# PSUM banks sorted by the engine that empties them, and rounds of segment attention and retention in another order

## Chip, core and metric

The kernel runs on one core of one Trainium2 chip. The metric is the device time of one execution in microseconds. Five engines work in parallel, each through its own instruction stream in order: TensorE (PE, matmuls and transposes, with its weight loads shown as PEld), VectorE (DVE), ScalarE (ACT), GpSimd (POOL) and SyncE (SP, DMA issue). Matmul results land in PSUM, which has eight banks; an engine has to empty a bank before TensorE writes the next result to it.

## What is computed

A four layer decoder on x of shape (16, 256, 128) with a context of shape (16, 64, 128). Each layer is attention (of a different kind each time), cross attention to the context, and a feed forward part, each followed by a residual add and layer norm. All of it is float32. The parts that the change touches, in the reference's words, cut to what matters:

```python
# layer 0, 2, 3: cross attention, 16 heads of 8, softmax over the 64 context positions
out = softmax(q @ k.T / sqrt(8)) @ v ;  x = layernorm(x + out @ Wo + bo)
# layer 1: attention in segments of 64, plus strided keys of two neighbour segments on either side
out = _attn(q, k, v)
for off in (1, 2):
    for sign in (-1, 1):
        out = out + where(valid, _attn(q, kd[n], vd[n]) * w, 0)
# layer 2, feed forward: int8 product
acc = dot(round(x / lhs_scale), round(rhs / rhs_scale));  x = layernorm(x + acc * lhs_scale * rhs_scale)
# layer 3: retention
qk = (qr @ kr.T) * mask;  out = (qk / clip(abs(sum(qk)), 1)) @ v
x = layernorm(x + (silu(x @ Wg + bg) * groupnorm(out)) @ Wo + bo)
```

## The kernel before

x stays in SBUF as 8 groups g of 512 tokens (two of the 16 batches b each): `xt` holds tokens on the partitions, `xT` the transpose. `transposed(g)` (L350) turns a group: four TensorE transposes to a bank, one copy to `xT` on ACT. Matmuls go through `mm` (L336), transposes through `tr` (L343), so nearly all TensorE work is shown under these two lines; the name of the output tile tells it apart.

Each stage is one `with s.banks(...)` block. `banks(tag=(n, k))` gives n buffers of k banks to a tag, and `bank(tag)` takes the next one in turn: a matmul that writes it waits for the last reader of what was there before. `in_order()` keeps TensorE's instructions in program order, so a waiting matmul holds up all that is behind it. `deferring()` puts off the last part of a layer norm until `settle()`.

**Segment attention** (`layer_a1`, the loop at L992). One round handles one batch. Its parts: own scores (segment keys; tag sc, exponentials on ACT as `eo`), far sums, sums (tags den, num), far scores (exponentials `e`), values (tag m, added on DVE to `vxs`, L904), project (tag m, q or k of a later group, evacuated by ACT), scaled (scores of the reciprocal, multiplied on DVE into `e`, L963), transposed, out (tag m, then the tail: DVE `r`, layer norm), and keys (POOL, `kb` L888). There is one m bank.

**Cross attention** (`layer_x0` for layer 0, which also hosts a recurrence by `side`, and two further users in layers 2 and 3). One round per batch: scores, then queries, sums, keys, out, values and transposed in some rounds. Banks before: sc 2 of 2 banks, nd few, m 4 - few, with few = 1 in layer 0 and 2 in the others. m takes values (emptied by DVE, `vx`), queries (DVE, `qT`), out (DVE, `r`), the recurrence's turn (DVE) and transposed (ACT, `xT`). Layer 3 begins with a mask row loaded by DMA, reduced on DVE to `nmx` (L1750).

**Int8 product and retention** (`Int8Product`, `layer_a3`). The loop runs over batches n with two half rounds t = 0, 1; g = n // 2. Four half rounds make a period, called H0 (n even, t 0), H1 (n even, t 1), H2 (n odd, t 0), H3 (n odd, t 1) here. Each has the next half's `scores` (tag sc; DVE multiplies into `a`, L1620), `outputs` (tag o), and some of: keys_values (`vz`, DVE), state (a transpose of k, copied by ACT to `kt`), state_product (`st`, DVE L1609), turned (two matmuls, DVE `tq`/`tk` and `ts`), integers (rounding), product (transposes of the rounded group, ACT copy `qT`, matmul, ACT `ys`, POOL, then DVE `r`), scales, gated (two matmuls and two Silu on ACT), normed, finish, transposed. All but scores and outputs use tag m, 3 banks.

Of the kernel before, what the change touches and what calls it, by code (L numbers as in the profile page):

```python
# [222 lines left out]
class Net:  # L223
# [125 lines left out]

    def transposed(self, g, dve=False):  # L350

        ps = self.bank("m" if "m" in self.ps else "ps1")
        for j in range(4):
            self.tr(ps[:, 128 * j:128 * j + 128], self.xt[:, 4 * g + j, :])
        (self.nc.vector.tensor_copy if dve else self.nc.scalar.copy)(self.xT[:, 512 * g:512 * g + 512], ps)  # L355
# [167 lines left out]
def cross_attention(s, wq, wk, wv, wo, bq, bk, bv, finish, mask=None, side=None):  # L523
# [80 lines left out]
    few = 1  # L604
    if side is None:
        side, few = lambda b, late: None, 2
    with s.banks(sc=(2, 2), nd=(few, 1), m=(4 - few, 1)), s.in_order(), s.deferring():
        side(-1, False)
        for g in range(2):
            ps = s.bank("nd")  # L610
            s.mm(ps, wk, s.ctx2[:, 8 * g:8 * g + 8, 0, :])
            evac(s, kT[:, 512 * g:512 * g + 512], ps, bk)
        values(0)
        side(-1, True)
        queries(0)
        keys(0)
        keys(1)
        scores(0)
        for b in range(B + 6):
            if b + 1 < B:  # L620
                scores(b + 1)
            s.settle()
            side(b, False)
            if b % 2 == 0 and b + 2 < B:
                queries(b // 2 + 1)
            if b < B:
                sums(b)
            side(b, True)
            if b + 2 < B:
                keys(b + 2)  # L630
            if b % 2 == 0 and 2 <= b <= B:
                out(b // 2 - 1)
            if b % 4 == 1 and b + 3 < B:
                values(b // 4 + 1)
            if b % 2 == 1 and b >= 5 and b // 2 - 2 < NG:
                s.transposed(b // 2 - 2)
# [223 lines left out]
def layer_a1(s, w):  # L860
# [108 lines left out]
    def far_sums(b):  # L969
        for u in range(2):  # L970
            for i in range(4):
                s.mm(num[b][32 * i:32 * i + 32, 1, :], vxs[b % 2][:, 4, i, 32 * u:32 * u + 32], ed[b][:, i, u, :],
                     u == 0, u == 1)
        oT[b] = s.work("oTn", [128, S], bufs=3)
        nc.vector.tensor_tensor(oT[b], rw[b], num[b][:, 1, :], ALU.add)
# [7 lines left out]
    with s.banks(sc=(2, 2), den=(1, 1), num=(2, 1), m=(1, 1)), s.in_order(), s.deferring():  # L983
        project(q, "qT", 0, w["q"], w["bq"])
        project(k, "kTs", 0, w["k"], w["bk"])
        keys(0)
        keys(1)
        values(0)
        project(q, "qT", 1, w["q"], w["bq"])
        own_scores(0)  # L990
        far_scores(0)
        for b in range(B + 4):  # L992
            if b + 1 < B:
                own_scores(b + 1)
            if 1 <= b <= B:
                far_sums(b - 1)
            if b < B:
                sums(b)
            if b + 1 < B:
                far_scores(b + 1)  # L1000
                values(b + 1)
            s.settle()
            g = (b + 3) // 2
            if g < NG:
                project(*((k, "kTs", g, w["k"], w["bk"]) if b % 2 == 0 else (q, "qT", g, w["q"], w["bq"])))
            if b < B:
                scaled(b)
            if b % 2 == 1 and 3 <= b and b // 2 - 2 >= 0 and b // 2 - 2 < NG:
                s.transposed(b // 2 - 2)
            if b % 2 == 1 and 3 <= b <= B + 1:  # L1010
                out(b // 2 - 1)
            if b + 2 < B:
                keys(b + 2)


def layer_x1(s, w, gate):
# [459 lines left out]
class Int8Product:  # L1476
# [3 lines left out]
    def __init__(self, s, w):  # L1480
        self.s, nc = s, s.nc
        self.idb = s.lp.tile([128, 128], BF, name="idb")
        nc.vector.tensor_copy(self.idb, s.ident)
        self.sw = sw = s.lp.tile([128, D], FP, name="sw")
        nc.gpsimd.partition_all_reduce(sw, w, 128, bass_isa.ReduceOp.absmax)
        nc.vector.tensor_scalar(sw, sw, 1e-12, 1.0 / 127.0, ALU.max, ALU.mult)
        q = s.work("t2", [128, 4, D], bufs=1)[:, 0, :]
        nc.vector.reciprocal(q, sw)
        nc.vector.tensor_tensor(q, q, w, ALU.mult)
        nc.vector.tensor_scalar(q, q, -127.0, None, ALU.max)  # L1490
        nc.vector.tensor_scalar(q, q, 127.0, MAGIC, ALU.min, ALU.add)
        self.qw = s.lp.tile([128, D], BF, name="qw")
        nc.vector.tensor_scalar(self.qw, q, MAGIC, None, ALU.subtract)
        self.xq, self.sx = {}, {}

    def integers(self, g):

# [10 lines left out]
        self.xq[g] = s.work("xq2", [128, 4, D], BF)  # L1508
        nc.vector.tensor_scalar(self.xq[g], t, MAGIC, None, ALU.subtract)

    def product(self, g):
        s, nc = self.s, self.s.nc
        ps = s.bank("m", [128, 4, 128], BF)
        for j in range(4):
            s.tr(ps[:, j, :], self.xq[g][:, j, :], self.idb)
        qT = s.work("qT2", [128, 4, 128], BF)
        nc.scalar.copy(qT, ps)
        y = s.bank("m", [128, 4, D])
        for j in range(4):
            s.mm(y[:, j, :], qT[:, j, :], self.qw)  # L1520
        ys = s.work("ys2", [128, 4, D], bufs=1)
        for j in range(4):
            nc.scalar.activation(ys[:, j, :], y[:, j, :], AF.Identity, scale=self.sx[g][:, j:j + 1])
        nc.gpsimd.tensor_tensor(ys, ys, self.sw.unsqueeze(1).broadcast_to([128, 4, D]), ALU.mult)
        s.tail(g, ys, transpose=False)


def layer_a3(s, w):
# [64 lines left out]
    def state(n):  # L1593

        kk, qb = qk["k", n // 2][:, n % 2, :], qk["q", n // 2][:, n % 2, :]
        ps = s.bank("m")
        s.tr(ps[:, 0:128], kk[:, 0:128])
        kt = s.work("kt", [128, 128])
        nc.scalar.copy(kt, ps[:, 0:128])
        cum = s.work("cum", [128, S])  # L1600
        nc.vector.tensor_tensor_scan(cum, ones, kk, 0.0, ALU.mult, ALU.add)
        nc.gpsimd.tensor_tensor(qks[n % 6], cum, qb, ALU.mult)
        return kt
# [53 lines left out]
        nc.vector.reciprocal(z, z)  # L1657
        return z

    def gated(g):  # L1660
        gates[g] = s.work("gate", [128, 2, 2, S])
        for c in range(2):
            ps = s.bank("m", [128, 2, S])
            s.mm(ps, w["g"][:, 128 * c:128 * c + 128], s.xT[:, 512 * g:512 * g + 512])
            nc.scalar.activation(gates[g][:, :, c, :], ps, AF.Silu, bias=w["bg"][:, c:c + 1])

    def normed(n):
        r = slice(32 * (n % 4 // 2), 32 * (n % 4 // 2) + 32)
# [12 lines left out]
                s.mm(y[:, j, :], gates[g][:, j // 2, c, 128 * (j % 2):128 * (j % 2) + 128], wo[:, c, :], c == 0, c == 1)  # L1681
        s.tail(g, y, s.biased(g, w["r_bo"]), transpose=False)

    with s.banks(sc=(2, 2), o=(1, 1), m=(3, 1)), s.in_order(), s.deferring():
        f2.product(0)
        s.settle()
        f2.integers(2)
        f2.product(1)
        s.transposed(0)
        turned("k", 0, ck, sk)  # L1690
        turned("q", 0, cq, sq)
        f2.integers(3)
        s.settle()
        f2.product(2)
        s.transposed(1)
        keys_values(0)
        kt = state(0)
        scores(0, 0)
        state_product(0, kt)
        for n in range(B + 6):  # L1700
            g = n // 2
            for t in range(2):
                nxt = (n, 1) if t == 0 else (n + 1, 0)
                if nxt[0] < B:
                    scores(*nxt)
                if n < B:
                    outputs(n, t)
                s.settle()
                if t == 0 and n + 1 < B:
                    keys_values(n + 1)  # L1710
                    kt = state(n + 1)
                if t == 1 and n + 1 < B:
                    state_product(n + 1, kt)
                if n % 2 == 0 and g + 1 < NG:
                    turned(*(("k", g + 1, ck, sk) if t == 0 else ("q", g + 1, cq, sq)))
                if n % 2 == 0 and t == 0 and g + 4 < NG:
                    f2.integers(g + 4)
                if n % 2 == 0 and t == 1 and g + 3 < NG:
                    f2.product(g + 3)
                if n % 2 == 1 and t == 0 and g + 2 < NG:  # L1720
                    s.transposed(g + 2)

                if n % 4 == 0 and t == 0 and 4 <= n <= B:
                    rs[n // 4 - 1] = scales(n - 4)
                d = g - 2
                if 0 <= d < NG:
                    if n % 2 == 0 and t == 1:
                        gated(d)
                    if n % 2 == 1:
                        normed(2 * d + t)  # L1730
                if n % 2 == 0 and t == 0 and 0 <= g - 3 < NG:
                    finish(g - 3)
                if n % 2 == 1 and t == 1 and 0 <= g - 3 < NG:
                    s.transposed(g - 3)
# [279 lines left out]
```

## Time and profile before

| | us |
|---|---|
| runs | 2192.61, 2199.82, 2200.99 (median 2199.82) |
| profiled execution | 2195.37, span 2193.6 |

The busy time by engine in the stretches of the stages (us from the span's start):

| stage | stretch | length | PE | DVE | ACT | POOL | PE clock |
|---|---|---|---|---|---|---|---|
| cross attention, layer 0 | 56 to 180 | 124 | 94.2 | 84.9 | 65.8 | 49.1 | 0.87 |
| segment attention | 282 to 541 | 259 | 208.3 | 117.5 | 97.4 | 65.1 | 0.89 |
| cross attention, layer 2 | 1076 to 1178 | 102 | 85.3 | 63.3 | 50.9 | 36.9 | 0.88 |
| int8 product, retention | 1178 to 1490 | 312 | 250.7 | 219.4 | 80.5 | 131.3 | 0.87 |
| cross attention, layer 3 | 1490 to 1605 | 115 | 87.1 | 79.9 | 70.6 | 62.6 | 0.89 |

The other stages, some 1,281 us, are not touched. In lines of the profile, "[1.32 <-DVE vxs L904]" at the end means that the engine stood idle for 1.32 us before the instruction and that the instruction waited last for the one named. In a group's line the figures after the bar are its busy time in us, the mean ns of one instruction, and the idle time just before the group's instructions.

### The profile page before, as it was taken

Reading aid. Unit: us, or ns where it says so; the run is one execution under the profiler, and the core shown is the slowest. Engines: PE = TensorE matmul, PEld = TensorE weight load, DVE = VectorE, ACT = ScalarE, POOL = GpSimd, SP = SyncE. Lnnn points to the kernel's source line nnn. Section 1 sums busy time; section 2 is a strip of 40 time slices with the busy share of each in tenths; the row PEclk is TensorE's granted clock in tenths of the full one; section 3 lists DMA queues with packets and bytes.
Section 4 is the critical chain, followed back from the end, with each engine's and each line's share of the span. In section 5 each row is a group of like instructions: output and inputs, shape, how many; then the busy total and the mean of one; then the engine's idle time right before and its main releaser. Section 6 shows DMA issues by size and latency. Waiting matters only on the chain.

```text
span 2193.6 us, 38398 instructions
## 1 busy us (share of the span) xinstructions
PE 1782.1 (81%) x16059; PEld 1102.1 (50%) x16060; DVE 1131.9 (52%) x2808; ACT 855.2 (39%) x1267; POOL 810.2 (37%) x956
## 2 busy tenths in 40 slices
PE   5784378887899945939895788897879988999998
PEld 2451256655677733625552455664434434555554
DVE  4677624555366665145476777856825543322231
ACT  6465633442333311322354122224756753332231
POOL 2342232221344324764533334435546652211110
PEclk8797569998899965979996889988989999999999
DMA  3000000001011121440000000001000000000000
GB/s 115 4 3 21 1 2 3 3 3 46 1 30 30 62 62 26 86 100 1 6 2 33 1 1 1 2 2 63 2 1 1 2 1 0 6 5 5 5 10 10
DMA packets 45646, 41.52 MB, mean 19 GB/s; under 512 B 6881, under 2 KB 42145, under 8 KB 44833
## 3 DMA queue, kind: packets, MB, share of 16 engines
q1 hardware_dynamic: 35456, 31.22, 4.6%
q0 software_dynamic: 5632, 4.33, 1.5%
q10 hardware_dynamic: 4384, 3.52, 0.5%
q8 instruction: 126, 2.06, 0.4%
q14 instruction: 48, 0.39, 0.1%
HBM read 28.44 MB, written 10.62 MB: 18 GB/s over the span
## 4 chain that ended last, share of the span: by engine, by line
PE 59%; DVE 17%; POOL 9%; issue 7%; ACT 4%; DMA 1%; POOLq 0%; DVEq 0%; ACTq 0%; SPq 0%
PE p L336 14%; PE m L336 13%; PE sc L336 12%; PE y L336 6%; PE nd L336 3%; PE nd L340 3%; POOL rs L383 2%; PE den L340 2%; DVE st L393 2%; PE m L343 2%; POOL acc L1312 2%; PE num L336 2%; DVE r L458 1%; ACT xt L404 1%; DVE e L963 1%
## 5 line engine op out<-in xcount | busy, mean ns | idle before, releaser
L336 PE MATMUL p<-h,w_f 128*128 128x512 f32 x512 | 222.3, 593 | 0.6 <-DVE h L1814 0.6
L381 POOL TENSOR_SCALAR ve<-mv 128x4 f32<-128x4 f32 x128 | 30.8, 241 | 432.3 <-DVE mv L394 429.6
L343 PE MATMUL m<-ident,xt 128*128 128x128 f32 x448 | 87.4, 317 | 95.3 <-ACT xt L404 48.5
L336 PEld LDWEIGHTS p<-h,w_f 128*128 128x128 f32 x512 | 96.9, 190 | 119.9 <-issue 118.0
L1904 ACT ACTIVATE e<-sc 128x1024 f32<-128x1024 f32 x128 | 124.0, 1021 | 61.7 <-PE sc L336 59.5
L383 POOL TENSOR_TENSOR rs<-ve,nhalf 128x4 f32<-128x4 f32 x128 | 133.9, 1046 | 6.3
L336 PE MATMUL sc<-qT,kb 32*128 32x64 f32 (+1 forms) x1792 | 103.8, 356 | 26.9 <-POOL kb L888 7.9
L343 PEld LDWEIGHTS m<-ident,xt 128*128 128x128 f32 x448 | 58.1, 155 | 129.6 <-ACT xt L404 56.8
L393 DVE BATCH_NORM_STATS2 st<-r 128x6 f32<-128x128 f32 x480 | 119.4, 271 | 2.6
L435 POOL TENSOR_TENSOR xb<-xt,r_x 128x512 f32<-128x512 f32 x48 | 61.1, 1276 | 158.5 <-DVE r L1757 72.3
L404 ACT ACTIVATE xt<-r,nm,rs 128x128 f32<-128x128 f32 x176 | 72.5, 484 | 106.9 <-POOL nm L399 106.9
L355 ACT COPY xT<-m 128x512 f32<-128x512 f32 x104 | 59.6, 580 | 132.6 <-PE m L343 132.0
L336 PE MATMUL m<-xT,w_a 128*128 128x512 f32 x144 | 81.9, 684 | 25.5 <-DVE vxs L904 18.6
L336 PEld LDWEIGHTS sc<-qT,kb 32*128 32x128 f32 x1792 | 77.7, 208 | 48.7 <-issue 16.7
L1819 ACT ACTIVATE h<-p,w_f 128x512 f32<-128x512 f32 x64 | 44.0, 687 | 146.8 <-PE p L336 146.7
L1975 DVE RECIPROCAL rcT<-nd 128x256 f32<-128x256 f32 x48 | 83.9, 1749 | 30.7 <-PE nd L336 30.7
L407 DVE TENSOR_SCALAR xt<-r,mv,rs 128x128 f32<-128x128 f32 x208 | 66.7, 382 | 59.6 <-POOL rs L383 59.6
L1825 DVE TENSOR_TENSOR ys<-y,r_f 128x512 f32<-128x512 f32 x8 | 5.5, 692 | 175.4 <-PE y L336 175.4
L1620 DVE TENSOR_TENSOR a<-sc,cst 128x1024 f32<-128x1024 f32 x64 | 75.0, 1208 | 14.3 <-PE sc L336 14.1
L578 ACT ACTIVATE e<-sc 128x1024 f32<-128x1024 f32 x64 | 61.9, 1019 | 49.7 <-PE sc L336 49.7
L394 DVE BATCH_NORM_AGGREGATE mv<-st 128x2 f32<-128x6 f32 x512 | 80.9, 166 | 0.1
L336 PE MATMUL sc<-kb,kTs 32*128 32x512 f32 x512 | 79.0, 652 | 0.0
(425 smaller groups left out, 4116.3 us busy)
## 6 DMA issues: line engine op xcount, KB each, us to landing
acc<-xt SPq DMA_DIRECT2D x16, 256.0 KB, 2.6
mw<-in_moe SPq DMA_DIRECT2D x8, 512.0 KB, 4.2
yx<-acc SPq DMA_DIRECT2D x12, 256.0 KB, 3.4
w_f<-in_w_f SPq DMA_DIRECT2D x1, 2824.0 KB, 10.4
w_x<-in_w_x SPq DMA_DIRECT2D x1, 2336.5 KB, 9.5
xt<-in_x SPq DMA_DIRECT2D x8, 256.0 KB, 7.4
rows<-xn SPq DMA_DIRECT2D x8, 256.0 KB, 2.5
out_x<-xt SPq DMA_DIRECT2D x8, 256.0 KB, 2.3
```

What stands on the lines that cost most here:

```text
L336: self.put(self.nc.tensor.matmul(out=out, lhsT=lhsT, rhs=rhs, start=start, stop=stop))
L340: self.put(self.nc.tensor.matmul(out=out, lhsT=lhsT, rhs=rhs, start=start, stop=stop, skip_group_check=True))
L343: self.put(self.nc.tensor.transpose(out, in_, self.ident if ident is None else ident))
L383: nc.gpsimd.tensor_tensor(rs, ve, self.nhalf[:, :n], ALU.pow)
L393: nc.vector.bn_stats(st[:, j, :], r[:, j, :])
L394: nc.vector.bn_aggr(mv[:, j, :], st[:, j, :])
L404: ins, front = nc.scalar.activation(out[:, j, :], r[:, j, :], AF.Identity, bias=nm[:, j:j + 1], scale=rs[:, j:j + 1]), self.latest
L407: ins, front = nc.vector.tensor_scalar(out[:, j, :], r[:, j, :], mv[:, j, 0:1], rs[:, j:j + 1], ALU.subtract, ALU.mult), self.mark
L578: s.latest = nc.scalar.activation(eu, sc[h], AF.Exp, scale=8 ** -0.5)
L1620: s.mark = nc.vector.tensor_tensor(a[:, h, :, :], sc[h].rearrange("p i j k -> p (i j) k"), tri, ALU.mult)
L1904: nc.scalar.activation(e[:, 2 * h:2 * h + 2, :, :], sc[h], AF.Exp, scale=8 ** -0.5)
L1975: s.nc.vector.reciprocal(rc, nd[:, 1, :])
```

## The change

Three things. In cross attention and retention a second tag t takes the tiles that ACT empties, and m keeps those that DVE empties, with the number of banks divided between them. In the retention loop the int8 product is split: `turn` (transposes and copy) runs in H0, one half round ahead of `product`; and `gated` is split by column half: half 1 stays in H1, half 0 moves to H3 of the pair before, ahead of `transposed` there. In segment attention, project moves from behind values to behind far sums, keys from the end of the round to behind sums, and transposed from the odd rounds (ahead of out) to the following even ones.

```diff
@@ transposed
-        ps = self.bank("m" if "m" in self.ps else "ps1")
+        ps = self.bank("t" if "t" in self.ps else "m")
@@ cross_attention
-    with s.banks(sc=(2, 2), nd=(few, 1), m=(4 - few, 1)), s.in_order(), s.deferring():
+    with s.banks(sc=(2, 2), nd=(few, 1), m=(1, 1), t=(3 - few, 1)), s.in_order(), s.deferring():
@@ layer_a1
-        for b in range(B + 4):
+        for b in range(B + 5):
             if b + 1 < B:
                 own_scores(b + 1)
             if 1 <= b <= B:
                 far_sums(b - 1)
+            g = (b + 3) // 2
+            if g < NG:
+                project(*((k, "kTs", g, w["k"], w["bk"]) if b % 2 == 0 else (q, "qT", g, w["q"], w["bq"])))
             if b < B:
                 sums(b)
+            if b + 2 < B:
+                keys(b + 2)
             if b + 1 < B:
                 far_scores(b + 1)
                 values(b + 1)
             s.settle()
-            g = (b + 3) // 2
-            if g < NG:
-                project(*((k, "kTs", g, w["k"], w["bk"]) if b % 2 == 0 else (q, "qT", g, w["q"], w["bq"])))
             if b < B:
                 scaled(b)
-            if b % 2 == 1 and 3 <= b and b // 2 - 2 >= 0 and b // 2 - 2 < NG:
-                s.transposed(b // 2 - 2)
+            if b % 2 == 0 and 0 <= b // 2 - 3 < NG:
+                s.transposed(b // 2 - 3)
             if b % 2 == 1 and 3 <= b <= B + 1:
                 out(b // 2 - 1)
-            if b + 2 < B:
-                keys(b + 2)
@@ Int8Product
+    def turn(self, g):
+        s, nc = self.s, self.s.nc
+        ps = s.bank("t", [128, 4, 128], BF)
+        for j in range(4):
+            s.tr(ps[:, j, :], self.xq[g][:, j, :], self.idb)
+        self.qT[g] = s.work("qT2", [128, 4, 128], BF)
+        nc.scalar.copy(self.qT[g], ps)
+
     def product(self, g):
-        ps = s.bank("m", [128, 4, 128], BF)
+        y = s.bank("t", [128, 4, D])
         for j in range(4):
-            s.tr(ps[:, j, :], self.xq[g][:, j, :], self.idb)
-        qT = s.work("qT2", [128, 4, 128], BF)
-        nc.scalar.copy(qT, ps)
-        y = s.bank("m", [128, 4, D])
-        for j in range(4):
-            s.mm(y[:, j, :], qT[:, j, :], self.qw)
+            s.mm(y[:, j, :], self.qT[g][:, j, :], self.qw)
@@ layer_a3, state
-        ps = s.bank("m")
+        ps = s.bank("t")
@@ layer_a3, gated
-    def gated(g):
-        gates[g] = s.work("gate", [128, 2, 2, S])
-        for c in range(2):
-            ps = s.bank("m", [128, 2, S])
-            s.mm(ps, w["g"][:, 128 * c:128 * c + 128], s.xT[:, 512 * g:512 * g + 512])
-            nc.scalar.activation(gates[g][:, :, c, :], ps, AF.Silu, bias=w["bg"][:, c:c + 1])
+    def gated(g, c):
+        if c == 0:
+            gates[g] = s.work("gate", [128, 2, 2, S])
+        ps = s.bank("t", [128, 2, S])
+        s.mm(ps, w["g"][:, 128 * c:128 * c + 128], s.xT[:, 512 * g:512 * g + 512])
+        nc.scalar.activation(gates[g][:, :, c, :], ps, AF.Silu, bias=w["bg"][:, c:c + 1])
@@ layer_a3, loop (a turn stands ahead of each product before the loop as well)
-    with s.banks(sc=(2, 2), o=(1, 1), m=(3, 1)), s.in_order(), s.deferring():
+    with s.banks(sc=(2, 2), o=(1, 1), m=(2, 1), t=(1, 1)), s.in_order(), s.deferring():
...
                     turned(*(("k", g + 1, ck, sk) if t == 0 else ("q", g + 1, cq, sq)))
+                if n % 2 == 0 and t == 0 and g + 3 < NG:
+                    f2.turn(g + 3)
...
                     if n % 2 == 0 and t == 1:
-                        gated(d)
+                        gated(d, 1)
                     if n % 2 == 1:
                         normed(2 * d + t)
+                if n % 2 == 1 and t == 1 and 0 <= d + 1 < NG:
+                    gated(d + 1, 0)
                 if n % 2 == 0 and t == 0 and 0 <= g - 3 < NG:
                     finish(g - 3)
                 if n % 2 == 1 and t == 1 and 0 <= g - 3 < NG:
                     s.transposed(g - 3)
```

More of the change, by code (lines that the diff above doesn't have):

```diff
@@ L1493, in __init__ @@
         nc.vector.tensor_scalar(self.qw, q, MAGIC, None, ALU.subtract)
-        self.xq, self.sx = {}, {}
+        self.xq, self.sx, self.qT = {}, {}, {}
     def integers(self, g):
@@ L1682, in finish @@
         s.tail(g, y, s.biased(g, w["r_bo"]), transpose=False)
-    with s.banks(sc=(2, 2), o=(1, 1), m=(3, 1)), s.in_order(), s.deferring():
+    with s.banks(sc=(2, 2), o=(1, 1), m=(2, 1), t=(1, 1)), s.in_order(), s.deferring():
+        f2.turn(0)
         f2.product(0)
@@ L1687, in layer_a3 @@
         f2.integers(2)
+        f2.turn(1)
         f2.product(1)
@@ L1693, in layer_a3 @@
         s.settle()
+        f2.turn(2)
         f2.product(2)
```

## The prediction

> **What bounds it.** I read the page first: its chain of work and its costliest groups.
>
> ```profile
> PE 59%; DVE 17%; POOL 9%; issue 7%; ACT 4%; DMA 1%; POOLq 0%; DVEq 0%; ACTq 0%; SPq 0%
> L336 PE MATMUL sc<-qT,kb 32*128 32x64 f32 (+1 forms) x1792 | 103.8, 356 | 26.9 <-POOL kb L888 7.9
> L336 PE MATMUL m<-xT,w_a 128*128 128x512 f32 x144 | 81.9, 684 | 25.5 <-DVE vxs L904 18.6
> L1620 DVE TENSOR_TENSOR a<-sc,cst 128x1024 f32<-128x1024 f32 x64 | 75.0, 1208 | 14.3 <-PE sc L336 14.1
> ```
>
> TensorE carries most of the chain, but the matmuls do not change (each engine has the same instructions after as before, and no moved step issues a DMA). What can change is where TensorE stands still for a PSUM bank, and which wait then ends last. The third line names one such wait: 18.6 us for DVE's vxs, all in the segment attention. So I went stage by stage: busy time by stretch, the waits of that stretch, and the timeline of one steady round.
>
> **Segment attention (a1), 13 steady rounds of 13.5 to 14 us.** The timeline of one round (start, duration):
>
> ```profile
> 398.10 1.15 PE L336 MATMUL sc<-qT,kbd 32*128 32x256 f32 x16
> 399.27 1.94 ACT L929 ACTIVATE e<-sc 128x1024 f32<-128x1024 f32 x2 [3.15 <-PE sc L336]
> ...
> 400.14 1.13 DVE L904 TENSOR_TENSOR vxs<-m,r_a 64x160 f32<-64x160 f32 x4 [1.00 <-PE m L336]
> ...
> 401.41 1.10 PE L336 MATMUL m<-xT,w_a 128*128 128x512 f32 x2 [1.32 <-DVE vxs L904]
> 402.44 1.15 PE L336 MATMUL sc<-rcT,w_a 32*128 32x256 f32 x16
> ...
> 403.62 2.35 DVE L963 TENSOR_TENSOR e<-e,sc 128x1024 f32<-128x1024 f32 x2 [2.35 <-PE sc L336]
> ```
>
> Far scores, values, a wait of 1.32 for the one m bank, project, scaled scores; then DVE multiplies (e) and the next own scores wait for its end. Far scores to e is 5.52 us. The change puts project behind far_sums: its 1.10 us of PE stay, but outside this stretch, which should be compared as 5.52 - 1.10 = 4.42. The new order already stands in the rounds that have no project (b = 13):
>
> ```profile
> 495.94 1.15 PE L336 MATMUL sc<-qT,kbd 32*128 32x256 f32 x16
> ...
> 499.11 1.13 PE L336 MATMUL sc<-rcT,w_a 32*128 32x256 f32 x12 [0.21 <-ACT e L929]
> 499.89 2.35 DVE L963 TENSOR_TENSOR e<-e,sc 128x1024 f32<-128x1024 f32 x2 [0.78 <-PE sc L336]
> ```
>
> That is 3.95. So not the 1.32 is won: scaled now waits for ACT's exponentials, and 4.42 - 3.95 = 0.47 a round remains; 13 rounds (b = 0 to 12): **-6.1**. Project now runs where m is free; its evacuation and the POOL kb it feeds come some 8 us earlier in the round. The 7.9 us of kb waits in the second line above lie beside the wait for e that follows them, so nothing is taken for them.
>
> Odd rounds end with transposed, ACT's copy and out, and the own scores start behind out, not behind e: 419.93 against e's end at 419.48, and 503.07 against 502.24 for b = 13. With transposed in the even rounds, where the wait for e covers it, out follows scaled at once: 4 x 0.5 + 0.9 = **-2.9**. In the tail the old order ran transposed(6) at 531.11 to 532.74, its copy, and only then out(7) at 533.42; now out(7) needs only oTn, ready at 528.54. What follows (norm, transposed(7), the first x1 matmul at 541.59) comes 4.9 earlier less some queueing: **-4.5**. Sum for a1 **-13.5**; ends -8 (only half of the 0.47 and half of the tail) and -16 (kb waits counted once).
>
> **Cross attention banks.** In x0, m goes from 3 banks to 1 and t gets 2; turn, queries, out and values, all emptied by DVE, now queue for one bank. Queries(b = 2, 6, 10) must wait for DVE's vx: done at 115.82 where queries started at 115.25, so 0.6 each; and turn waits for the r of out (0.3), with nd behind it. 3 x 0.6 plus 0.2: **+2**, ends 0 (TensorE waits for xT or oTn anyway: 8.2 and 7.5 us of such waits in this stage) and +3.5.
>
> In x2 and x3, m goes from 2 to 1 and t gets 1. Queries(b = 6, 10) waited 0.6 for ACT's xT copy only because of its bank; that goes, about 0.9 each with the next instruction's lead. Against it, out now waits for qT's evacuation (x2, b = 8: qT ends 1131.94, out started 1131.28, +0.7; in x3 1530.28 against 1530.39, nothing). x2: -1.8 + 0.7, and at b = 4 up to 1.15 more (qT ends 1110.31, out started 1109.16): **0** (ends -1, +1.5); x3: **-1.9** (ends -2.5, 0).
>
> At x3's start the instruction order of DVE changes too. Before:
>
> ```profile
> 1497.88 1.22 DVE L1750 TENSOR_REDUCE nmx<-e 128x16 f32<-128x1024 f32 x1 [6.98 <-DMA e<-in_mk]
> ...
> 1499.24 2.63 DVE L554 TENSOR_TENSOR vx<-m,r_x 64x64 f32<-64x64 f32 x8
> ...
> 1501.90 0.75 DVE L644 TENSOR_SCALAR qT<-m,w_x 128x512 f32<-128x512 f32 x1
> 1502.80 2.09 PE L336 MATMUL sc<-qT,kb 32*128 32x256 f32 x16 [6.25 <-DVE qT L644]
> ```
>
> In the changed build the eight vx stand ahead of nmx, in the 6.98 us that DVE waits for the mask. Then 1497.88 + 1.22 + 0.75 + 0.15 = 1500.0 for the scores: **-2.7** (ends -3, and 0 if what follows waits for another transfer).
>
> **Retention with the int8 product (a3).** A period is two batches, four half rounds H0 to H3, 33.4 us, about seven of them; DVE (219 of 312 us) and POOL between its parts set it. m goes from 3 to 2, and t (1 bank) takes everything that ACT empties: state's transpose, transposed, turn, product, gated.
>
> ```profile
> DVE r L458 <- POOL ys L1524: 20.5, 6, 4.1
> ...
> DVE a L1620 <- PE sc L336: 14.1, 12, 3.5
> PE m L343 <- DVE st L1609: 11.2, 5, 3.4
> ```
>
> The columns are total, times, longest. H1: the wait of 3.4 for st in front of the product's transposes goes, since turn ran in H0; but with two m banks the ts matmul takes over the same wait for st. ts comes 0.5 later, ys 0.7 ahead of the second qk, and the next DVE work stands behind r, which waits 4.1 for POOL's ys: -0.2 a period, five periods, **-1**. So the largest wait that this part removes is worth almost nothing.
>
> H3: gated(c = 0) now stands ahead of transposed(g-3), and both use the one t bank. TensorE pays 0.95 for gated's two matmuls and then waits for the Silu (0.69) and some 0.2 of latency: 1.85. Behind it stand the scores for which DVE's next a waits:
>
> ```profile
> 1377.38 0.66 PE L343 MATMUL m<-ident,xt 128*128 128x128 f32 x4
> ...
> 1379.17 2.36 DVE L1620 TENSOR_TENSOR a<-sc,cst 128x1024 f32<-128x1024 f32 x2 [0.25 <-PE sc L336]
> ```
>
> a waited already (0.25 here, 0.93 in two others), so the 1.85 lands on the chain: four periods with transposed x 1.85 and two without it x 0.8, **+9**. H0: ts behind vz and scales, finish behind ts: +0.3 to 1.5 on PE, under the 4 us before the next a, and 0.5 with the prologue. Sum **+8.5**; ends 0 (DVE catches up where it idles anyway) and +11.
>
> The Trainium skill speaks against this part: Perfetto Trace Analysis, Optimizing Tensor Performance, Matmuls, wants independent matmul groups rotated through different banks, so that one's evacuation overlaps the next group. Eight tiles a period now pass through t, with evacuations of 2 x 0.27 (kt), 3 x 0.58 (xT, qT), 1.14 (ys) and 2 x 0.69; with 0.2 latency each, 6.4 us a period, some 45 us by the rule if all were exposed. By the rows only the pair gated, transposed stands together on the chain; I take the rows. A second rule: TensorE: Matmul & The Clock Gate, Why this matters for your kernels, warns that idle gaps above about 3 us drop the clock. The trace agrees: after that 3.36 wait four matmuls of the ts/gate form took 3.72 us, against 1.88 at 1321.85. If the gap went, the rule would give 1.84 x 5 = 9 us; but ts waits in the same place, and DVE's r waits for POOL until 1332.43 whatever PE does. I take 0.
>
> **Sum.** -13.5 + 2 + 0 - 1.9 - 2.7 + 8.5 = **-7.6**. The profiled execution took 2195.4 (span 2193.6 and 1.8 around it), so 2187.8; the median of the runs is 4.4 higher, and with the same difference I forecast **2192**. About 0.5%, 11 us, is what a measurement of this kernel can tell from no change.
>
> **Rivals.**
> 1. *The waits added in a3 are covered* (a3 0): For it: DVE is busy 23 to 29 of each 33 us, and most of its idle time is spent on POOL, not PE. Against: a waits for PE's scores twelve times. -7.6 - 8.5 = -16: **2184**.
> 2. *Slower: the one t bank of a3 chains TensorE to ACT.* TensorE works in order, so each reuse of t stops everything behind it, and ACT's part may itself stand behind four scaled copies (1.14) or a table load (1.28, at 1365.75). Exposed in each period: turn to product 0.8, product to gated 1.3, gated to transposed 1.85, kt 0.5, ts behind vz 0.2: 4.65, over seven periods +33 in place of 8.5: +17, **2217**. It decides from about 3.8 us a period (a3 at +27). Against: three of these pairs have other PE work between them.
> 3. *a1's order gives nothing*: the 0.47 is eaten because project's evacuation on ACT delays the exponentials behind it. a1 then keeps 2.9 and 4.5: -7.6 + 6.1 = -1.5: **2198**.
>
> **Chances.** Forecast 0.42 (own range 2184 to 2200, of it 0.10 faster by over 11 us), rival 1 0.25 (0.23 faster), rival 2 0.20 (0.18 slower), rival 3 0.13 (0.03 slower). Together faster 0.33, same 0.46, slower 0.21. The range: 2176 is rival 1 with a1 at -16 and x2, x3 and x0 at their lower ends (-5.6 more); 2212 leaves out the last third of rival 2.
>
> **What would show it.** a1: the group m<-xT,w_a loses its wait for vxs; scaled waits for ACT e instead; rounds 0.5 shorter; x1's first matmul near 528. x2, x3: TensorE's waits for ACT xT shrink; x3's scores follow the mask within 3 us. a3: a new wait of TensorE for the gate's Silu before transposed, DVE's wait for sc up from 14.1 to over 20, the retention stage some 8 us longer. I am wrong if a3 is over 15 us longer or no longer at all, or if a1 shortens by less than 8.

## The result, and the profile after

The changed kernel is slower: median 2212.93 us against 2201.14 us before (12 runs each), ratio 1.0042 with a 95% interval of 1.0026 to 1.0058, some 9 us. Its profiled execution has a span of 2205.3 us, 11.7 more than the one of before. The page of the changed kernel, its chain and two groups:

```profile
PE 58%; DVE 18%; POOL 9%; issue 7%; ACT 5%; DMA 1%; POOLq 0%; DVEq 0%; ACTq 0%
...
L336 PE MATMUL m<-xT,w_a 128*128 128x512 f32 x112 | 73.2, 748 | 25.5 <-DVE st L1612 21.6
L1623 DVE TENSOR_TENSOR a<-sc,cst 128x1024 f32<-128x1024 f32 x64 | 75.0, 1208 | 21.2 <-PE sc L336 21.0
```

The idle time in front of m<-xT,w_a is the same 25.5 us as before, but its cause has moved: vxs (segment attention) is gone, and st (retention) stands in its place. The group has 32 matmuls less, those of gated, which are now in tag t; the mean of those left is 748 ns, against 684 in the larger group before. DVE's a waits 21.0 us for scores instead of 14.1.

Lengths of stages, read from the first or last instruction of a named tile in each trace (us). The runs below the line are the experiments; "3 banks" means retention with m 3 as before.

| kernel | x0 | segment attention | x1 | to x2 | x2 | retention loop | its tail | x3 | rest |
|---|---|---|---|---|---|---|---|---|---|
| before | 227.5 | 251.7 | 259.1 | 279.8 | 98.6 | 277.3 | 43.6 | 112.3 | 578.5 |
| after | 228.5 | 240.3 | 259.6 | 280.5 | 101.0 | 293.2 | 48.7 | 109.0 | 578.4 |
| | | | | | | | | | |
| a1_only | 227.6 | 240.8 | 259.0 | 284.4 | 98.9 | 280.9 | 43.6 | 112.1 | 578.2 |
| cross_only | 229.8 | 254.8 | 259.5 | 283.6 | 101.3 | 275.3 | 43.6 | 114.5 | 582.1 |
| a3_only | 227.6 | 248.4 | 258.9 | 283.7 | 98.3 | 295.8 | 48.5 | 112.5 | 582.1 |
| old_a3 | 228.4 | 240.6 | 259.4 | 283.6 | 101.1 | 282.0 | 43.2 | 115.0 | 581.5 |
| gate_back | 229.8 | 240.9 | 259.8 | 279.9 | 96.1 | 300.4 | 42.9 | 109.4 | 582.0 |
| gate_behind | 228.9 | 235.8 | 259.8 | 279.8 | 96.0 | 298.0 | 47.2 | 108.5 | 581.4 |
| order_alone (3 banks) | 228.3 | 240.0 | 259.6 | 279.8 | 96.3 | 272.5 | 45.5 | 114.1 | 581.9 |
| banks_alone | 229.6 | 240.0 | 259.6 | 279.2 | 100.0 | 306.3 | 43.7 | 108.4 | 583.1 |
| best (3 banks) | 228.5 | 232.3 | 259.5 | 284.3 | 98.6 | 273.4 | 45.4 | 111.8 | 581.3 |
| gate0_in_m | 230.1 | 241.0 | 259.6 | 283.6 | 101.2 | 292.9 | 46.5 | 108.7 | 581.5 |
| turn_only (3 banks) | 227.7 | 240.3 | 259.6 | 283.6 | 98.7 | 267.9 | 43.5 | 111.9 | 581.5 |
| gate_only (3 banks) | 228.1 | 243.7 | 259.5 | 287.0 | 98.4 | 286.1 | 44.8 | 112.7 | 578.5 |

The retention loop runs from the int8 weights' absolute maximum (sw) to the last sqr, its tail from there to the reduction of the mask. X0 includes what follows up to the first values of segment attention, and "to x2" and "rest" are stages whose code no kernel changes. So one reads at once how far a single trace can be trusted: "rest" has either 578.2 to 578.5 or 581.3 to 583.1, "to x2" 279.2 to 287.0, and segment attention in its new order 232.3 to 243.7. Most of this goes with the granted clock. TensorE runs the same 3,000 instructions in the same order in "rest" of before and of cross_only; over its first 10 us the granted clock was 0.80 in the one and 0.50 in the other, and the same two matmuls took 1.12 and 2.08 us. Segment attention took 232.3 us at a mean clock of 0.93 (best), 240 to 241 at 0.90 to 0.91, and 243.7 at 0.89 (gate_only). Differences of 3 to 4 us in one stage of one trace are therefore nothing, and 8 can be. The gain of segment attention stands above that: all eleven traces of the new order lie under the three of the old one (248.4 to 254.8). So does the loss of the retention: after and a3_only lie above all four traces of the old retention, in the loop and in its tail.

The two places of the prediction's retention part, in the timeline of the changed kernel. H1:

```profile
1363.02 0.42 DVE L1612 TENSOR_TENSOR st<-m,cst 128x256 f32<-128x256 f32 x1
...
1363.49 2.08 PE L336 MATMUL m<-xT,w_a 128*128 128x512 f32 x2 [3.04 <-DVE st L1612]
...
1365.61 0.75 DVE L1581 SCALAR_TENSOR_TENSOR ts<-m,w_a 128x512 f32<-128x512 f32 x1 [1.51 <-PE m L336]
...
1367.29 2.08 PE L336 MATMUL t<-xT,w_a 128*128 128x512 f32 x2 [1.29 <-ACT ys L1526]
...
1369.76 1.20 DVE L458 TENSOR_TENSOR r<-ys,xt 128x512 f32<-128x512 f32 x1 [3.40 <-POOL ys L1527]
```

With two m banks the ts matmuls wait 3.04 us for st, as predicted; here they take 2.08 us behind it (granted clock 0.50) where the pair before them took 1.02 at 1359.43; DVE's ts itself now waits 1.51 for them, and gated waits another 1.29 for ys to leave the t bank. H3:

```profile
1380.98 1.12 PE L336 MATMUL t<-xT,w_a 128*128 128x512 f32 x2
...
1382.20 0.69 ACT L1668 ACTIVATE gate<-t,w_a 128x512 f32<-128x512 f32 x1 [1.70 <-PE t L336]
1382.94 0.66 PE L343 MATMUL t<-ident,xt 128*128 128x128 f32 x4 [0.84 <-ACT gate L1668]
...
1384.74 2.35 DVE L1623 TENSOR_TENSOR a<-sc,cst 128x1024 f32<-128x1024 f32 x2 [2.89 <-PE sc L336]
```

Gated, its Silu, and only then transposed; DVE's a waits 2.89 where it waited 0.25. This is the chain that was predicted. Over the whole retention loop two further waits have grown or are new. The first row is from before, the others from the changed kernel (total, times, longest):

```profile
DVE ts L1578 <- PE m L336: 0.6, 1, 0.6
...
DVE ts L1581 <- PE m L336: 10.2, 15, 1.5
...
PE t L336 <- ACT ys L1526: 3.9, 3, 1.3
```

The wait of ts comes with m, which has two banks now; the wait for ys is that for the one bank of t.

### The profile page after: what moved, and what is told of

It is laid out like the page before. It is cut to its first block, busy times and chain, and to the rows that moved or that the text cites. A ratio compares the mean times of both kernels' runs of the same rounds, so it can differ in the third digit from the quotient of the medians.

```text
span 2205.3 us, 38402 instructions
## 1 busy us (share of the span) xinstructions
PE 1805.9 (82%) x16060; PEld 1103.2 (50%) x16060; DVE 1141.4 (52%) x2808; ACT 857.7 (39%) x1268; POOL 811.2 (37%) x956
## 4 chain that ended last, share of the span: by engine, by line
PE 58%; DVE 18%; POOL 9%; issue 7%; ACT 5%; DMA 1%; POOLq 0%; DVEq 0%; ACTq 0%
PE p L336 14%; PE m L336 13%; PE sc L336 12%; PE y L336 6%; PE nd L340 3%; PE nd L336 3%; POOL rs L383 2%; PE den L340 2%; POOL acc L1312 2%; DVE rcT L1985 2%; DVE e L963 2%; DVE st L393 1%; PE num L336 1%; PE o L340 1%; DVE r L458 1%
## 5 line engine op out<-in xcount | busy, mean ns | idle before, releaser
L1914 ACT ACTIVATE e<-sc 128x1024 f32<-128x1024 f32 x128 | 124.0, 1021 | 61.6 <-PE sc L336 59.5
L343 PE MATMUL m<-ident,xt 128*128 128x128 f32 x256 | 50.7, 321 | 61.1 <-ACT xt L404 34.5
L336 PE MATMUL m<-xT,w_a 128*128 128x512 f32 x112 | 73.2, 748 | 25.5 <-DVE st L1612 21.6
L578 ACT ACTIVATE e<-sc 128x1024 f32<-128x1024 f32 x64 | 61.9, 1018 | 55.5 <-PE sc L336 55.5
L435 POOL TENSOR_TENSOR xb<-xt,r_a 128x512 f32<-128x512 f32 x24 | 30.7, 1282 | 136.0 <-DVE r L458 134.8
L1088 ACT ACTIVATE e<-sc 128x1024 f32<-128x1024 f32 x32 | 32.8, 1024 | 110.0 <-PE sc L336 110.0
```

The costliest lines, as they stand in the source:

```text
L336: self.put(self.nc.tensor.matmul(out=out, lhsT=lhsT, rhs=rhs, start=start, stop=stop))
L435: self.nc.gpsimd.tensor_tensor(t, self.xt[:, 4 * g:4 * g + 4, :], row.unsqueeze(1).broadcast_to([128, 4, D]), ALU.add)
L578: s.latest = nc.scalar.activation(eu, sc[h], AF.Exp, scale=8 ** -0.5)
L1914: nc.scalar.activation(e[:, 2 * h:2 * h + 2, :, :], sc[h], AF.Exp, scale=8 ** -0.5)
```

## The experiments

**First: do the parts add up?** Theory A: they do, and the loss sits in the retention. Theory B: it is made by what the other parts do to its start. Each kernel takes the parts named from the changed kernel and all else from before.

```diff
# a1_only: layer_a1's loop alone
# cross_only: transposed's tag and
+    with s.banks(sc=(2, 2), nd=(few, 1), m=(1, 1), t=(3 - few, 1)), s.in_order(), s.deferring():
# a3_only: transposed's tag, Int8Product and layer_a3 alone
# old_a3: all but Int8Product and layer_a3
```

> Only the round order of segment attention is changed; banks everywhere and the retention are as before. Theory A (the parts add up; the loss sits in the retention stage): segment attention ends 11 us earlier, the rest of the kernel just follows, so about 11 us faster than before, ratio 0.995. Theory B (the gain of segment attention is lost again downstream, because later stages wait for transfers or for the clock whatever its end): under 5 us faster, ratio 0.998 to 1.000, with the first matmul of the next stage still about 10 us earlier.

Measured: ratio 0.9957 (0.9942 to 0.9972), as theory A expected. Segment attention 240.8.

> Only the banks of the three cross attentions are changed (m 1, t 2 or 1). Theory A: +1 in layer 0, +2.4 in layer 2 as in the trace of the changed kernel, -3 in layer 3: 0 to +1 us, ratio 1.000. Theory B (single m bank is what costs, and layer 3's gain needs the later arrival that the slow retention gave it): +3 us or more, ratio 1.0015 or above.

Measured: 1.0061 (1.0037 to 1.0085), on the side of theory B.

> Only the int8 product and retention are changed (banks m 2, t 1, turn in H0, gated half 0 in H3). Theory A: the stage is some 21 us longer by itself, ratio 1.009 to 1.010. Theory B (part of those 21 us came from where the other parts moved the start of the stage): +8 to +14 us, ratio 1.004 to 1.006.

Measured: 1.0116 (1.0084 to 1.0148), near what theory A expected. Loop and tail 344.3 against 320.9.

> Segment attention and cross attention banks changed, int8 product and retention as before. Theory A: -11 from segment attention, 0 to +1 from the cross attentions: 10 to 11 us faster than before, ratio 0.995, and 20 us below the changed kernel. Theory B: no more than 5 us faster, ratio 0.998 to 1.000.

Measured: 0.9972 (0.9955 to 0.9989), between the two theories: the interval leaves out the 0.995 of A and takes in the 0.998 of B.

Theory A holds for where the two large parts lie: the segment order keeps its gain by itself, and the retention part loses some 23 us by itself. That the parts add up is not shown. Alone they sum to -0.43 + 0.61 + 1.16 = +1.34%, and together they gave +0.42%, some 20 us less; 5.5 of these lie in x3 (below), the others are not placed. A's expectation for the cross attention banks missed: they cost something in a kernel in which nothing else is changed. Of the 13 us by the ratio, the stages show about 7 (x0 +2.3, x2 +2.7, x3 +2.2), and the rest cannot be placed. In pairs of kernels that differ in nothing else the cost is smaller, 3 us (old_a3 against a1_only) and 6 us (order_alone against best, further down). In x3 the sign depends on the order that the build gives DVE. Where the eight vx stand behind the mask's reduction, as in cross_only, old_a3 and order_alone, queries wait for vx in the single m bank; the waits of TensorE in order_alone:

```profile
PE m L336 <- DVE vx L554: 7.0, 1, 7.0
```

Where vx stand ahead of it, as in the changed kernel, the mask no longer holds anything up, and the scores follow its reduction in 2.15 us instead of 4.92:

```profile
1507.80 1.27 DVE L554 TENSOR_TENSOR vx<-m,r_x 64x64 f32<-64x64 f32 x8 [2.02 <-POOL vx L535]
...
1513.04 1.22 DVE L1760 TENSOR_REDUCE nmx<-e 128x16 f32<-128x1024 f32 x1 [3.96 <-DMA e<-in_mk]
...
1515.19 2.09 PE L336 MATMUL sc<-qT,kb 32*128 32x256 f32 x16 [4.42 <-DVE qT L644]
```

**Second: what in the retention?** Theory P: the pair gated, transposed in H3. Theory Q: the banks, through ts and the clock. All start from the changed kernel, but banks_alone, which starts from old_a3.

```diff
# gate_back: gated whole in H1, in t
+                        gated(d, 0)
                         gated(d, 1)
-                if n % 2 == 1 and t == 1 and 0 <= d + 1 < NG:
-                    gated(d + 1, 0)
# gate_behind: the last two lines placed behind s.transposed(g - 3)
# order_alone: every "t" of the retention and int8 product is "m"
+    with s.banks(sc=(2, 2), o=(1, 1), m=(3, 1)), s.in_order(), s.deferring():
# banks_alone: the old order, with the tags of the changed kernel
+    with s.banks(sc=(2, 2), o=(1, 1), m=(2, 1), t=(1, 1)), s.in_order(), s.deferring():
```

> The changed kernel with gated's half 0 back in H1, ahead of half 1 (both in the one t bank); turn stays split off. Theory P (the pair gated, Silu, transposed in H3 is what costs, in the loop and in the stage's tail): the retention stage goes from 342 us (from sw to the reduction of the mask) to 327 or less; all in all 12 to 16 us below the changed kernel, ratio to before about 0.998. Theory Q (two m banks: ts stands behind st and its matmuls then run at half clock): the stage falls by 5 us at most, ratio to before 1.002 or more.

Measured: 1.0060 (1.0033 to 1.0086). Loop and tail 343.3: no shorter.

> The changed kernel with gated's half 0 still in H3, but behind transposed there, so transposed does not wait for the Silu. Theory P: of the 2 us in each H3 the wait of 0.84 and its latency go and gated's own 1 us of TensorE stays; the tail's 5 us go: the stage 8 to 11 us shorter, ratio to before about 1.000. Theory Q: 3 us shorter at most.

Measured: 1.0039 (1.0024 to 1.0054). Loop and tail 345.2: no shorter.

> The changed kernel, but int8 product and retention use one tag m with three banks, as before; only the order of turn and gated is new there. Theory P, read strictly: with three banks in turn neither transposed waits for the Silu nor ts for st, only gated's 1 us of TensorE in H3 is left: the stage 14 to 17 us shorter than 342, ratio to before 0.997 to 0.998. If the order itself (gated in H3, POOL's gate ahead of the norm in the tail) is the cause: 6 us shorter at most.

Measured: 0.9978 (0.9963 to 0.9993), a ratio that P, read strictly, had named as well. Loop and tail 318.0, some 24 us shorter, more than P expected.

> Segment attention and cross attention as changed, int8 product and retention in the old order, but with banks m 2 and t 1. Theory P: H3 and the tail are as of old; ts behind st and the chain product, gated, gated through t in H1 cost 1 to 1.5 us a period: the stage 6 to 10 us longer than the 322 of the old one, ratio to before 1.000 to 1.002. Theory Q: the banks are the cause: 15 us longer or more, ratio 1.005 or above.

Measured: 1.0089 (1.0061 to 1.0117), as theory Q expected. Loop and tail 350.0.

To see where in the period the time goes, take the distance from one start of DVE's a to the next in each timeline and sum it by kind of half round: the last seven of the eight that cross H1, and the last four that cross H3 (the earlier four differ by up to 3.6 us in sum between the traces with the old retention).

| | before | after | gate_back | gate_behind | banks_alone | order_alone | gate0_in_m | best | turn_only | gate_only |
|---|---|---|---|---|---|---|---|---|---|---|
| across H1, 7 steps | 64.6 | 65.7 | 82.2 | 68.1 | 87.0 | 57.2 | 66.7 | 58.2 | 59.6 | 61.9 |
| across H3, last 4 | 18.7 | 28.8 | 21.4 | 29.9 | 21.4 | 21.9 | 23.8 | 22.1 | 17.7 | 21.5 |

Theory P falls as the main cause. Gate_back takes away the pair in H3 (28.8 to 21.4) and the tail's loss (42.9), but pays 16.5 in H1, where product, gated and gated now follow each other through the one bank. Gate_behind gains nothing: in one bank the second of the pair waits, whichever it is. Order_alone and banks_alone decide: with the new order, three rotating banks in place of m 2, t 1 are worth 293.2 + 48.7 - 272.5 - 45.5 = 24 us; with the old order the new banks cost 350.0 - 322.4 = 28 us (322.4 is the mean of before, a1_only, cross_only and old_a3, which share the old retention and span 318.9 to 325.2). By the ratios of the whole kernels the same pairs give 14 us (after against order_alone) and 26 us (banks_alone against old_a3); in both the kernel with the new banks also has the other order of DVE in x3, which takes 5 to 7 us off it there. Of theory Q the banks are shown, its clock is not: the loop took 282.0 us in old_a3, 292.9 in gate0_in_m (below) and 300.4 in gate_back, all at a mean clock of 0.84. Nor do the runs say which half of the split costs more, two banks for m or one for t: DVE's wait for ts (10.2 to 11.6 us with the new banks in either order, 0.6 or less with three) belongs to the first, the waits for Silu and ys to the second.

The order itself gains 7 us across H1 and gives 3 back in H3 and 2 in the tail. Loop and tail come to 318.0, hardly below the 318.9 to 325.2 of the old order, and by the ratio order_alone is no faster than old_a3 (0.9972), from which it differs in this order alone. Two rows of banks_alone, DVE's waits in this stage:

```profile
DVE a L1620 <- PE sc L336: 29.8, 19, 6.6
DVE r L458 <- POOL ys L1524: 22.2, 7, 4.1
```

Scores came late 19 times instead of 12, for 29.8 us.

**Third: the pair in H3 alone, and a better kernel.**

```diff
# gate0_in_m: the changed kernel, with
-        ps = s.bank("t", [128, 2, S])
+        ps = s.bank("m" if c == 0 else "t", [128, 2, S])
         s.mm(ps, w["g"]...
# best: order_alone, with the banks of cross attention as before
+    with s.banks(sc=(2, 2), nd=(few, 1), m=(4 - few, 1)), s.in_order(), s.deferring():
```

> The changed kernel, only gated's half 0 (the one in H3) takes a bank of m; all else in t as changed. If sharing the one t bank with transposed is what costs in H3, TensorE's waits for the gate's Silu (5.0 us) go and the steps from H3 to H0, 10 us longer than before in the changed kernel, come back to 2 to 4 us longer; the stage 6 to 8 us shorter than 342, ratio to before about 1.001. If gated's own time on TensorE is what costs there, the steps stay 8 us or more above.

Measured: 1.0001 (0.9983 to 1.0019). The waits for the gate's Silu are gone; the four H3 steps fall from 28.8 to 23.8. So of the 10.1 us there, 5.0 are the shared bank, about 3 are gated's own matmuls (21.9 and 22.1 with three banks), and 2 are not placed. The stage missed its expectation: 339.4 in place of 341.9, not 6 to 8 us less, as the first four H3 steps of this trace were 3.5 us longer; the ratio met it.

> Banks everywhere as before the change; the new order in segment attention and the new order of turn and gated in the retention. Theory O (the order gains and the banks lose): segment attention 11 us shorter, retention 2 to 5 us shorter, the cross attentions as of old: 11 to 16 us faster than before, ratio 0.993 to 0.995, the fastest of all. Rival (the new order of the retention only looked good by a lucky clock): no faster than with the segment order alone, ratio 0.9957 or above.

Measured: 0.9952 (0.9936 to 0.9969), with theory O; but its interval covers a1_only's 0.9957, so the new retention order as a whole is not separated from the rival, and the stage (318.8 for loop and tail against 318.9 to 325.2) does not do it either.

**Last: which half of the retention's order gains?** Both from best.

```diff
# turn_only: gated whole in H1
+                        gated(d, 0)
                         gated(d, 1)
-                if n % 2 == 1 and t == 1 and 0 <= d + 1 < NG:
-                    gated(d + 1, 0)
# gate_only: turn in H1, in front of product
-                if n % 2 == 0 and t == 0 and g + 3 < NG:
-                    f2.turn(g + 3)
+                    f2.turn(g + 3)
                     f2.product(g + 3)
```

> Banks everywhere as of old, the new round order in segment attention; in the retention only turn is moved to H0, gated stays whole in H1. If the earlier turn is what the new retention order gains (TensorE's wait for st then stands in front of less), the steps from H1 to H2 are 6 to 7 us shorter in sum than before, the tail is the old 43.6, ratio 0.993 to 0.995. If it is the lighter H1 (gated's half 0 moved out), the H1 to H2 steps are at most 2 us shorter.

Measured: 0.9881 (0.9831 to 0.9931), from few runs and so with a wide interval; 2183.65 us median, the shortest of all, with 311.4 for loop and tail; the interval lies below a1_only's.

> As the run turn_only, but with only gated split and its half 0 moved to H3; turn stays with product in H1. If the earlier turn is the gain: H1 to H2 steps at most 2 us shorter than before, H3 to H0 about 3 us longer, the tail 45.5, ratio 0.996 to 0.997. If the lighter H1 is the gain: H1 to H2 5 us shorter or more, ratio 0.995.

Measured: 0.9970 (0.9953 to 0.9988); 330.9 for loop and tail, of which some 6 us lie in the first four H3 steps and are not placed.

The earlier turn is the gain: across H1 59.6 (5 of the expected 6 to 7), the tail as of old, and H3 without loss. Moving gated costs 3 in H3 and 1 to 2 in the tail for 2.7 in H1. One period of turn_only suggests why turn helps once there are three banks:

```profile
1344.20 1.88 PE L336 MATMUL m<-xT,w_a 128*128 128x512 f32 x4
1348.27 0.58 PE L336 MATMUL m<-qw,qT 128*128 128x128 bf16 x4 [2.18 <-DVE st L1612]
1348.93 3.32 PE L336 MATMUL m<-xT,w_a 128*128 128x512 f32 x4
1352.17 1.17 PE L336 MATMUL sc<-tq,kb 32*128 32x128 f32 x32
```

Tq's and ts's matmuls run together, in 1.88 us, before st; only the product stands behind st. The gate matmuls are slow in this period (3.32 us) but delay nobody: DVE waits for POOL's ys and is busy with r and its norm until 1354.50, and the scores are done at 1353.34.

## Why the prediction was wrong

It forecast -7.6 us on the profiled execution; that came out at +11.7. The median, forecast at 2192, was 2212.93. Step by step, as forecast and as in the two traces:

| | forecast | measured |
|---|---|---|
| segment attention | -13.5 | -11.4 |
| x0 | +2 | +1.0 |
| x2 | 0 | +2.4 |
| x3, start and loop | -4.6 | -3.3 |
| retention, loop and tail | +8.5 | +21.0 |
| stages not touched | 0 | +2.0 |

**The step that failed is the retention's sum, +8.5, where +21.0 was measured.** That is over the 15 us that the prediction itself named as a sign of being wrong. Three terms of it:

- *"By the rows only the pair gated, transposed stands together on the chain; I take the rows."* The pair was right. That its size came out so well, +9 forecast and +9.4 over all H3 steps, is in part luck: the four steps with transposed cost 10.1 where 7.4 was forecast, the earlier ones nothing where 1.6 was. But the choice of rows over the Trainium skill's rule (Perfetto Trace Analysis, Optimizing Tensor Performance, Matmuls: rotate independent groups through different banks) was wrong. I priced each bank wait by the order of before, in which other work stands between the pairs, and for H1 took one net figure for order and banks. The traces of before, order_alone and after take it apart: the order gains 7.4 us across H1, the banks lose 8.5 there, 6.9 in H3, 2.4 across H0, and 3 in the tail; with the first periods 24 us in all. That is half of the 45 that the prediction estimated from the rule with every evacuation exposed, and not the +8.5 of the rows.
- *"ts comes 0.5 later"*, inside the -1 for H1. The prediction saw that ts would take over the wait for st, but not what that does to DVE: ts waited for its matmuls fifteen times, 10.2 us in all, against 0.6 once before. The net of H1 came out at +1.1 against -1. The clock, for which it says *"I take 0"*, adds to this only at times: in the period shown the two ts matmuls took 2.08 us in place of 1.02, but of the seven matmuls that came first behind the wait for st in this trace (1.94 to 3.73 us) two took 1.22 us, one 0.78 and four 0.70. The prediction's "The trace agrees" was too much as well: in its own trace, after the other wait of 3.36 us at 1393.69, the four matmuls took 1.98 us at a granted clock of 1.00.
- *The tail was not priced at all.* Once no more batches start, gated's half 0 and transposed follow each other with nothing between: the Silu at 1483.06, transposed at 1483.80, and finish's matmuls only at 1484.71. Tail lengths are 42.9 to 43.7 in every kernel with gated whole in H1, whatever the banks; 44.8 to 45.5 with half 0 in H3 and three banks; 46.5 to 48.7 with half 0 in H3 and the new banks. So the move costs 1 to 2 and the banks up to 3.

**Segment attention** was right in kind. The group's wait for vxs is gone, and the tail's gain is there (from the last oTn to the next stage's first transfer 5.9 us in place of 11.4, so -5.5 where -4.5 was forecast). The rounds gained 5.9, not 9.0. I had said of kb's earlier start only that nothing is taken for it. It has a price:

```profile
400.32 1.89 POOL L888 TENSOR_TENSOR kb<-kTs,cst 128x1024 f32<-128x1024 f32 x1
400.74 1.76 DVE L944 TENSOR_TENSOR rcT<-rcT,w_a 128x256 f32<-128x256 f32 x1
...
402.64 1.36 PE L336 MATMUL sc<-rcT,w_a 32*128 32x256 f32 x16 [0.95 <-DVE rcT L944]
```

DVE's product rcT took 0.42 to 0.43 us in all rounds before; now POOL's kb runs beside it in seven of the sixteen rounds, and it takes 1.52 to 1.89 and ends just behind kb. Scaled waits for it, 8.1 us in total against 1.5 before. The Trainium skill (SBUF — State Buffer, SBUF: two separate sides) calls the port pair of DVE and GpSimd an exclusive lock: of a DVE instruction with two SBUF inputs and a GpSimd one that reads SBUF, whichever starts first has it for the whole instruction. These durations agree. No run here took that collision away, and 3 us in one stage is within what the clock does, so how much of the missing 3 us is owed to it stays open.

**Cross attention.** x0's +2 (+1.0 measured) and x3's start (-2.7 forecast, 4.92 to 2.15 measured) hold. X2's 0 cannot be judged: with the new banks x2 took 100.0 to 101.3 at a granted clock of 0.89 to 0.91 and 96.0 to 96.3 at 0.96, with the old ones 98.3 to 98.9 at 0.90 to 0.92.

**The rivals.** Rival 2 named the t bank, which is one half of what decided (the two banks of m are the other), and put the retention at +33 where +21 was measured; the segment gain then held the whole to +0.4%. Rival 1 fell, since DVE's wait for scores grew from 14.1 to 21.0 us and loop and tail by 21, and rival 3, since a1_only alone is 0.43% faster.

## What to carry to other kernels

- When an edit changes banks and order together, price them apart: the order with the old banks, and the banks with the old order. Here the order was worth some 4 us at most (11 with turn moved alone), and the banks cost 24 to 28 in the same stage; a net figure hid both.
- Splitting a small pool by the engine that empties it takes the slack out of rotation. In a pool of one bank TensorE waited for the reader in either order of the pair (28.8 and 29.9 us across H3, 21.9 with three in rotation), and with two in place of three DVE's ts waited 10.2 us in place of 0.6.
- After an idle gap ask which matmuls come first, since they may run slow, and put there what nobody waits for.
- Before a stage of one trace is compared with another, compare the granted clock of the two.

## What had not been expected of the hardware

- The same DVE instruction took 0.42 us alone and 1.52 to 1.89 beside POOL's kb.
- Behind some waits of 2 to 3 us the next matmuls took about double: 2.08 against 1.02 us for a pair of 512 columns, and a little later 2.09 against 1.17 for the 32 of the scores. Not behind all: of the 22 gaps of 2 to 3.5 us in the trace of the changed kernel, 12 were followed by a matmul at a granted clock of 0.5 to 0.6 and 10 by one at 0.8 to 1.0.
- Stages whose code is the same took one of a few lengths, some 3 to 4 us apart, in different kernels, and the granted clock differed with them. The reading of one trace is no finer than that unless several kernels share the stage.
